# Two steps at a time in media attention and local attention of a decoder kernel on one core

## The chip, the core and the metric

The kernel runs on one core of one Trainium2 chip. The core has a matrix engine (TensorE, PE in the profile, with its weight loads as PEld), three engines for element-wise work (VectorE or DVE, ScalarE or ACT, GpSimd or POOL), and a queue that issues transfers (SyncE or SP). TensorE reads SBUF and writes PSUM, the accumulator memory; VectorE and ScalarE read PSUM. The metric is the time of one execution on the device in microseconds (us), lower is better. Of the kernel before there are three timed runs and one profiled execution.

## The reference, cut to what matters

The reference is two decoder layers on an input `x` of 8 batches of 512 rows and 256 columns, all in 32-bit floats. In order: self-attention, cross-attention to a context, two local transformer layers (each local attention and a feed-forward part), an attention in integers, an attention to the context as "media", and a mixture of eight experts. Each adds its result to `x`. The change touches two of them.

Local attention has 8 heads of 64 columns. A row attends to its own block of 128 rows and the block before:

```python
sim = jnp.einsum('bhwid,bhwjd->bhwij', bq, bk)
sim = jnp.where(mask, -jnp.finfo(sim.dtype).max, sim)
attn = jax.nn.softmax(sim, axis=-1)
out = jnp.einsum('bhwij,bhwjd->bhwid', attn, bv)
```

Queries and keys are normalised and rotated by position ahead of this. Media attention also has 8 heads of 64 columns; all 512 rows attend to all 512 rows of the context that the mask leaves:

```python
attn = jax.nn.softmax(sim, axis=-1)
out = jnp.einsum('bhij,bhjd->bhid', attn, v)
return out @ Wout
```

## The kernel before, in words

The stages run one after the other, with the beginning of each woven into the end of the one before. `x` stays in SBUF. Both attentions work transposed: keys stand on the partitions and queries along the columns, so that the exponentials are the operand of the value product as they come.

**A step.** Heads go in pairs, `c` = 0 to 3, since two heads of 64 fill 128 partitions. In media attention a step is a batch `b`, a pair of heads `c` and a block of 128 keys `kt`: 8 x 4 x 4 = 128 steps. In local attention it is a batch, a pair of heads and a half of the key blocks: 8 x 4 x 2 = 64 steps in each of two layers.

**Scores** (`scores`, lines 1912 and 2805). The two heads of a pair lie on the upper and the lower 64 partitions, so a score matmul uses 64 rows of the array, and the two run at once on two halves of its rows. They go to a PSUM tile `sc` of two banks, of which there are two. In media attention ScalarE takes the exponential from PSUM to `ma_e` (line 2817, four tiles), and the exponentials are summed over the key blocks in `ma_esum`: GpSimd copies the first (line 2823), VectorE adds the others (line 2825). In local attention VectorE adds the mask on the way from PSUM to `la_e` (line 1929, six tiles), and ScalarE takes the exponential in place (line 1933).

**Value products** (`weigh`, lines 1945 and 2827) take a step's exponentials two steps later. Each head has 64 value columns, so the two heads use two halves of the array's columns, and write the upper and lower half of one PSUM bank `po`, of which there is one. After the last step of a head pair ScalarE copies `po` out (lines 1962 and 2843). After two head pairs, sums over the exponentials are formed on 32-column tiles into the bank `sum` (recorded under lines 1940 and 2854), copied by VectorE, sent out through two small transfers, inverted (`inverted`, line 3162), spread over partitions by transfers into `x_wide` and multiplied on GpSimd (`times_rows`, line 3180). Media attention's last batch does the division on the chip instead (`spread_sums`).

**The rest.** Between steps stand two kinds of other work. `prepare` yields the next batch's work in small pieces: in media attention loads and normalisation, two groups of transposes (line 2784) and four projections of the queries (line 2794); in local attention two groups of transposes of `x` (`turn`, line 1796, copied by ScalarE to `la_hT`), twelve projections (line 1812), a rotation of queries and keys for each of four row tiles on VectorE (`rotate`, lines 1824 to 1846: some twenty instructions from the reduction `la_ss` to the last sum into `la_qk`), and the transposes of the rotated rows (`turn_heads`, line 1855, copied to `la_qkT`). All go through two PSUM banks `pj`. The other kind is `later`, a list of work with a delay counted in ticks: the inversion, the multiplication, the output projection (lines 1988 and 2892), and in media attention the routing for the experts (lines 2970 to 3063). `tick(n)` runs up to n pieces that are due.

**The order.** The loop of a stage is written out for all its steps:

```python
scores(i)
weigh(i - 2)

```

The order on each engine is made from this by a planner: on an engine the instruction that was written earliest goes first among those that are ready by the planner's estimate of times, so that an instruction that it thinks not ready is passed by later ones. At run time an engine does its instructions in the planned order and waits where one is not ready. `together(n)` (line 1448) wraps a group of matmuls: the first takes its place in the order, and the others follow it with the highest priority.

Of the kernel before, what the change touches and what calls it, by code (L numbers as in the profile page):

```python
# [27 lines left out]
F32 = mybir.dt.float32  # L28
# [5 lines left out]
AF = mybir.ActivationFunctionType  # L34
ALU = mybir.AluOpType
# [4 lines left out]
P = 128  # L40
B, S, C = 8, 512, 256
NST = S // P
# [1235 lines left out]
class FastDecoder(Decoder):  # L1278
# [480 lines left out]
    def local_attention(self, l, y, ahead):  # L1759
# [130 lines left out]
        with self.tc.tile_pool(  # L1890
# [11 lines left out]
            mask = self.alloc(pool, [P, NST, P], F32, "la_mask", bufs=1)  # L1902
# [7 lines left out]
            mask = mask.rearrange("p j k -> p (j k)")  # L1910

            def scores(n):
                b, rest = divmod(n, 8)
                c, half = divmod(rest, 2)
                d = held[b]
                ps = self.alloc(psum, [P, 2, 512], F32, "sc", bufs=2)
                for m in self.together(4):
                    jj, r = divmod(m, 2)
                    j = 2 * half + jj
                    to = min((j + 2) * P, S)  # L1920
                    rows = slice(64 * r, 64 * r + 64)
                    nc.tensor.matmul(  # L1922
                        ps[:, r, jj * 256 : jj * 256 + to - j * P],
                        d["qkT"][rows, 4 + c, j * P : (j + 1) * P], d["qkT"][rows, c, j * P : to],
                        start=True, stop=True,
                    )
                n_cols = 384 if half else 512
                ex = self.alloc(pool, [P, 2, 512], F32, "la_e", bufs=6)
                nc.vector.tensor_tensor(  # L1929
                    ex[:, :, :n_cols], ps[:, :, :n_cols],  # L1930
                    mask[:, :n_cols].unsqueeze(1).broadcast_to([P, 2, n_cols]), ALU.add,
                )
                nc.scalar.activation(ex[:, :, :n_cols], ex[:, :, :n_cols], AF.Exp, scale=-1.0)  # L1933
                d["e", rest] = ex

            def over_keys(out, lhsT, ex, half, jj):

# [5 lines left out]
                )  # L1943

            def weigh(n):
                b, rest = divmod(n, 8)
                c, half = divmod(rest, 2)
                d = held[b]
                if half == 0:
                    d["po"] = self.alloc(psum, [P, 512], F32, "po")  # L1950
                ex = d["e", rest]
                for m in self.together(4):
                    jj, r = divmod(m, 2)
                    at = 128 * c + 64 * r
                    over_keys(
                        d["po"][64 * r : 64 * r + 64, :], lambda j: d["v"][:, j, at : at + 64],
                        ex[:, r, :], half, jj,
                    )
                if half == 0:
                    return  # L1960
                o = d["o", c] = self.alloc(pool, [P, S], F32, "la_o", bufs=3)
                nc.scalar.copy(o, d["po"])  # L1962
                if c % 2 == 0:
                    return
                ps = self.alloc(psum, [P, 512], F32, "sum")
                for m in self.together(16):
                    hf, jj, r = m // 8, m // 4 % 2, m % 4
                    over_keys(
                        ps[32 * r : 32 * r + 32, :], lambda j: self.ones[:, :32],
                        d["e", 2 * (c - 1 + r // 2) + hf][:, r % 2, :], hf, jj,  # L1970
                    )
                total = self.alloc(pool, [P, S], F32, "la_total")
                nc.vector.tensor_copy(total, ps)
# [20 lines left out]

            n = 8 * B
            ahead.step()
            for i in range(n + 2):
                if i < n:
                    if i % 8 == 0:
                        ready = prepare(i // 8 + 1) if i // 8 + 1 < B else [()] * 8  # L2000
                    scores(i)
                if i >= 2:
                    weigh(i - 2)
                later.tick(1)
                if i < n:
                    for thunk in ready[i % 8]:
                        thunk()
                        later.tick(1)
                if i == n - 6:
                    early.close()  # L2010
                if i > n - 6:
                    ahead.step()
            ahead.step(100)
            later.drain()

# [732 lines left out]
    def stage_media_attention(self, w, out):  # L2748


        nc, t = self.nc, self.t
        wq, wkv, wo = w
        later = Background()
        with self.tc.tile_pool(reuse_waits="tile", name="ma", bufs=2) as pool, self.tc.tile_pool(
# [48 lines left out]
                    yield lambda g=g: project(d["q"], wq, d["xnT"], g)  # L2803

            def scores(n):
                b, rest = divmod(n, 16)
                c, kt = divmod(rest, 4)
                d = held[b]
                ps = self.alloc(psum, [P, 2, 512], F32, "sc", bufs=2)
                for r in self.together(2):  # L2810
                    rows = slice(64 * r, 64 * r + 64)
                    nc.tensor.matmul(  # L2812
                        ps[:, r, :], d["k"][rows, c, kt * P : (kt + 1) * P], d["q"][rows, c, :],
                        start=True, stop=True,
                    )
                ex = self.alloc(pool, [P, 2, 512], F32, "ma_e", bufs=4)
                nc.scalar.activation(  # L2817
                    ex, ps, AF.Exp, bias=bias[:, b * NST + kt : b * NST + kt + 1], scale=0.125
                )
                d[rest] = ex  # L2820
                if kt == 0:
                    d["sum", c] = self.alloc(pool, [P, 2, 512], F32, "ma_esum", bufs=3)
                    nc.gpsimd.tensor_copy(d["sum", c], ex)
                else:
                    nc.vector.tensor_tensor(d["sum", c], d["sum", c], ex, ALU.add)  # L2825

            def weigh(n):
                b, rest = divmod(n, 16)
                c, kt = divmod(rest, 4)
                d = held[b]  # L2830
                if kt == 0:
                    d["po"] = self.alloc(psum, [P, 512], F32, "po")
                ex = d.pop(rest)
                for r in self.together(2):
                    nc.tensor.matmul(  # L2835
                        d["po"][64 * r : 64 * r + 64, :],
                        d["v"][:, kt, 128 * c + 64 * r : 128 * c + 64 * r + 64], ex[:, r, :],
                        start=(kt == 0), stop=(kt == 3),
                    )
                if kt < 3:  # L2840
# [11 lines left out]
                ps = self.alloc(psum, [P, 512], F32, "sum")  # L2852
# [49 lines left out]
                thunk()  # L2902
            n = 16 * B
            ready = None
            for i in range(n + 2):
                if i < n:
                    if i % 16 == 0:
                        for thunk in ready or ():
                            thunk()
                        ready = prepare(i // 16 + 1) if i // 16 + 1 < B else iter(())  # L2910
# [534 lines left out]
```

## Time and profile before

| | |
|---|---|
| median of 3 runs | 3174.21 us (3169.55 to 3178.64) |
| profiled execution: time, span | 3162.05 us, 3160.1 us |
| TensorE matmuls | 2877.0 us, 91% of the span |
| VectorE | 2166.9 us, 69% |
| ScalarE | 1154.0 us, 37% |
| GpSimd | 408.7 us, 13% |
| granted TensorE clock, mean | 0.973 |

Shares are of the whole span; the stages differ. Local attention runs at about 740 to 1200 us and 1455 to 1905 us, media attention at about 2455 to 2885 us. A 32-bit matmul shows as two records, so the 256 score matmuls of media attention are 512 records of line 2812, and a step's group of two is four. A matmul's length in the profile contains its way through the array and its end is modelled: what a group costs is read from the start of one to the start of the next. In the rows of the profile a name such as `sc<-ma_qT,ma_kT` gives the tile written and the tiles read, and "64\*128" the rows and columns of the array in use.

### The profile page before, as it was taken

To read this page: it belongs to the slowest core of one execution; us is meant where nothing else is said; L and a number is where in the kernel's file an instruction comes from. 1 tells how busy PE (TensorE), PEld (TensorE's weight loads), DVE (VectorE), ACT (ScalarE), POOL (GpSimd) and SP (SyncE) were. 2 spreads that over 40 slices of the span, in tenths; PEclk is the share of its full clock that TensorE was granted. 3 is DMA by queue.
4 is the path that set the end of the run, shared out by engine and by line. 5 is a ranking of instruction groups with operands and counts; after the bars stand their busy time and mean duration, and the time that the engine had idled before them with its cause. 6 is when DMAs were issued, how large, how long until landed. Compare 5 with 4: busy or idle time off the path is not lost. (4 is left out here: it accounts for less than half of the span.)

```text
span 3160.1 us, 40243 instructions
## 1 busy us (share of the span) xinstructions
PE 2877.0 (91%) x14929; PEld 1485.8 (47%) x14944; DVE 2166.9 (69%) x4962; ACT 1154.0 (37%) x1607; POOL 408.7 (13%) x389
## 2 busy tenths in 40 slices
PE   8998888877998989999988989998796999997998
PEld 5642222224555556655555546654444233333665
DVE  7458888887788795357788798558787766566110
ACT  2146556653434431123434431113353444342111
POOL 1111000000011010000101111111201122222111
PEclk9999999989999999999999999999997999998999
DMA  7011111111000001001000011001332122213331
GB/s 237 1 53 44 54 57 48 32 24 51 16 21 22 19 27 42 0 1 35 22 15 21 22 44 61 15 12 60 95 127 94 41 79 103 75 64 103 102 138 59
DMA packets 130695, 168.73 MB, mean 53 GB/s; under 512 B 51760, under 2 KB 79665, under 8 KB 128442
## 3 DMA queue, kind: packets, MB, share of 16 engines
q1 hardware_dynamic: 126394, 154.48, 15.6%
q0 software_dynamic: 4096, 11.59, 1.0%
q8 instruction: 119, 1.95, 0.3%
q14 instruction: 86, 0.70, 0.1%
HBM read 113.12 MB, written 47.50 MB: 51 GB/s over the span
## 5 line engine op out<-in xcount | busy, mean ns | idle before, releaser
L1812 PE MATMUL pj<-w,la_hT 128*128 128x512 f32 x720 | 345.3, 612 | 23.9 <-DVE la_v L1817 21.9
L1664 DVE TENSOR_TENSOR x_e<-x_e,x_share 128x1024 f32<-128x1024 f32 x256 | 309.1, 1253 | 25.1 <-ACT x_e L1663 24.3
L1663 ACT ACTIVATE x_e<-sc 128x1024 f32<-128x1024 f32 x256 | 249.7, 1026 | 147.9 <-PE sc L1652 145.5
L2817 ACT ACTIVATE ma_e<-sc,ma_bias 128x1024 f32<-128x1024 f32 x128 | 142.4, 1114 | 198.8 <-PE sc L2812 185.5
L1812 PEld LDWEIGHTS pj<-w,la_hT 128*128 128x128 f32 x720 | 129.5, 191 | 167.0 <-issue 119.0
L3188 POOL TENSOR_TENSOR la_oT<-la_o,x_wide 128x512 f32<-128x512 f32 x64 | 96.8, 1523 | 790.6 <-DMA x_wide<-invs 654.6
L2825 DVE TENSOR_TENSOR ma_esum<-ma_esum,ma_e 128x1024 f32<-128x1024 f32 x96 | 122.8, 1280 | 91.6 <-ACT ma_e L2817 90.9
L1933 ACT ACTIVATE la_e<-la_e 128x1024 f32<-128x1024 f32 (+1 forms) x128 | 121.4, 951 | 175.2 <-DVE la_e L1929 175.2
L2146 ACT ACTIVATE lf_gate<-pj,lf_b 128x512 f32<-128x512 f32 (+1 forms) x82 | 56.3, 687 | 338.1 <-PE pj L2125 327.1
L1679 PE MATMUL po<-x_e,x_v 128*32 128x512 f32 x1024 | 140.1, 620 | 37.2 <-DVE x_e L1664 34.1
L2125 PE MATMUL pj<-lf_hnT,w 128*128 128x512 f32 (+1 forms) x368 | 171.9, 595 | 1.2 <-DVE lf_hid L2151 1.1
L1929 DVE TENSOR_TENSOR la_e<-sc,la_mask 128x1024 f32<-128x1024 f32 (+1 forms) x128 | 138.3, 1081 | 38.8 <-PE sc L1922 38.8
L1652 PE MATMUL sc<-x_q,x_k 32*128 32x512 f32 x1024 | 159.2, 662 | 0.3 <-ACT x_e L1663 0.2
L2125 PE MATMUL sc<-lf_hnT,w 128*128 128x512 f32 x336 | 158.0, 592 | 0.0
L2197 PE MATMUL po<-w,lf_hid 128*128 128x256 f32 x640 | 148.9, 379 | 0.2 <-DVE x L2207 0.2
L1988 PE MATMUL pj<-w,la_oT 128*128 128x256 f32 x512 | 124.4, 389 | 23.4 <-ACT la_qkT L1858 12.6
L2812 PE MATMUL sc<-ma_qT,ma_kT 64*128 64x512 f32 x512 | 145.2, 644 | 0.0
L2151 DVE SCALAR_TENSOR_TENSOR lf_hid<-sc,lf_b,lf_gate 128x512 f32<-128x512 f32 x70 | 52.4, 748 | 126.3 <-PE sc L2125 126.3
L2835 PE MATMUL po<-ma_e,ma_v 128*64 128x512 f32 x512 | 138.1, 618 | 0.0
L1940 PE MATMUL po<-la_e,la_v 128*64 128x256 f32 (+1 forms) x1024 | 129.1, 374 | 6.4 <-ACT la_o L1962 6.3
L1922 PE MATMUL sc<-la_qkT 64*128 64x256 f32 (+1 forms) x1024 | 132.6, 378 | 1.3 <-DVE la_e L1929 1.3
L1819 ACT ACTIVATE la_sq<-pj 128x512 f32<-128x512 f32 x120 | 71.4, 595 | 156.2 <-PE pj L1812 155.9
(491 smaller groups left out, 5264.5 us busy)
## 6 DMA issues: line engine op xcount, KB each, us to landing
x_wide<-invs SPq DMA_DIRECT2D x184, 128.0 KB
w<-in_f_w_dram SPq DMA_DIRECT2D x16, 1024.0 KB
kv<-kv_o SPq DMA_DIRECT2D x56, 256.0 KB
slots<-x_empty SPq DMA_DIRECT2D x8, 1028.0 KB
x_mask<-in_x_maskT_dram SPq DMA_DIRECT2D x8, 1024.0 KB
ma_kT<-kv SPq DMA_DIRECT2D x8, 1024.0 KB
ma_v<-kv SPq DMA_DIRECT2D x8, 1024.0 KB
ex_rows<-slots SPq DMA_DIRECT2D x7, 1028.0 KB
```

What stands on the lines that cost most here:

```text
L1652: nc.tensor.matmul(pair[r // 2][:, r % 2, :], d["k"][rows, g, kt * P : (kt + 1) * P], d["q"][rows, e, g, :], start=True, stop=True,)
L1663: nc.scalar.activation(ex, d["e"][rest][p], AF.Exp)
L1664: nc.vector.tensor_tensor(ex, ex, d["share"][:, kt, :].unsqueeze(1).broadcast_to([P, 2, 512]), ALU.mult)
L1679: nc.tensor.matmul(d["po"][32 * r : 32 * r + 32, :], d["v"][:, kt, 8 * g + 2 * r + e, :], ex[r // 2][:, r % 2, :], start=(kt == 0), stop=( ...
L1812: nc.tensor.matmul(ps, d["hT"][:, k, i * P : (i + 1) * P], wqkv[:, k, j * S : (j + 1) * S], start=(k == 0), stop=(k == 1),)
L1922: nc.tensor.matmul(ps[:, r, jj * 256 : jj * 256 + to - j * P], d["qkT"][rows, 4 + c, j * P : (j + 1) * P], d["qkT"][rows, c, j * P : to], ...
L1929: nc.vector.tensor_tensor(ex[:, :, :n_cols], ps[:, :, :n_cols], mask[:, :n_cols].unsqueeze(1).broadcast_to([P, 2, n_cols]), ALU.add,)
L2125: nc.tensor.matmul(ps[:m, :], w1[:, k, at : at + m], held[b]["hnT"][:, k, :], start=(k == 0), stop=(k == 1))
L2197: nc.tensor.matmul(ps[:, :C], held[b]["hid"][:, f, i * P : (i + 1) * P], w2[:, f, :], start=(f == 0), stop=False,)
L2812: nc.tensor.matmul(ps[:, r, :], d["k"][rows, c, kt * P : (kt + 1) * P], d["q"][rows, c, :], start=True, stop=True,)
L2817: nc.scalar.activation(ex, ps, AF.Exp, bias=bias[:, b * NST + kt : b * NST + kt + 1], scale=0.125)
L2835: nc.tensor.matmul(d["po"][64 * r : 64 * r + 64, :], d["v"][:, kt, 128 * c + 64 * r : 128 * c + 64 * r + 64], ex[:, r, :], start=(kt == 0) ...
```

## The change

Steps are taken in pairs. `scores` now takes the number of a pair, allocates both `sc` tiles at once, issues all matmuls of the two steps in one group, and then their mask additions, exponentials and sums. `weigh` takes the value products of both steps of the preceding pair in one group. In the loop the scores of a pair come first, then the value products of the pair before, and then the background pieces of both steps, with as many ticks as before. A pair is two key blocks of one head pair in media attention, and the two halves of one head pair in local attention. No tile is added, and no count of buffers changed. Of the diff, lines that only move in are left out:

```diff
@@ local_attention
             def scores(n):
-                b, rest = divmod(n, 8)
-                c, half = divmod(rest, 2)
+                b, c = divmod(n, 4)
                 d = held[b]
-                ps = self.alloc(psum, [P, 2, 512], F32, "sc", bufs=2)
-                for m in self.together(4):
-                    jj, r = divmod(m, 2)
+                both = [self.alloc(psum, [P, 2, 512], F32, "sc", bufs=2) for half in range(2)]
+                for m in self.together(8):
+                    half, jj, r = m // 4, m // 2 % 2, m % 2
                     j = 2 * half + jj
                     to = min((j + 2) * P, S)
                     rows = slice(64 * r, 64 * r + 64)
                     nc.tensor.matmul(
-                        ps[:, r, jj * 256 : jj * 256 + to - j * P],
+                        both[half][:, r, jj * 256 : jj * 256 + to - j * P],
                         d["qkT"][rows, 4 + c, j * P : (j + 1) * P], d["qkT"][rows, c, j * P : to],
                         start=True, stop=True,
                     )
+                for half, ps in enumerate(both):
+                    n_cols = 384 if half else 512
+                    ex = self.alloc(pool, [P, 2, 512], F32, "la_e", bufs=6)
...
             def weigh(n):
-                b, rest = divmod(n, 8)
-                c, half = divmod(rest, 2)
+                b, c = divmod(n, 4)
                 d = held[b]
-                if half == 0:
-                    d["po"] = self.alloc(psum, [P, 512], F32, "po")
-                ex = d["e", rest]
-                for m in self.together(4):
-                    jj, r = divmod(m, 2)
+                d["po"] = self.alloc(psum, [P, 512], F32, "po")
+                for m in self.together(8):
+                    half, jj, r = m // 4, m // 2 % 2, m % 2
...
-                if half == 0:
-                    return
...
             n = 8 * B
             ahead.step()
-            for i in range(n + 2):
-                if i < n:
-                    if i % 8 == 0:
-                        ready = prepare(i // 8 + 1) if i // 8 + 1 < B else [()] * 8
-                    scores(i)
-                if i >= 2:
-                    weigh(i - 2)
-                later.tick(1)
-                if i < n:
-                    for thunk in ready[i % 8]:
-                        thunk()
-                        later.tick(1)
-                if i == n - 6:
-                    early.close()
-                if i > n - 6:
-                    ahead.step()
+            for pair in range(0, n + 2, 2):
+                if pair < n:
+                    if pair % 8 == 0:
+                        ready = prepare(pair // 8 + 1) if pair // 8 + 1 < B else [()] * 8
+                    scores(pair // 2)
+                if pair >= 2:
+                    weigh(pair // 2 - 1)
+                for i in (pair, pair + 1):
+                    later.tick(1)
+                    if i < n:
+                        for thunk in ready[i % 8]:
+                            thunk()
+                            later.tick(1)
+                    if i == n - 6:
+                        early.close()
+                    if i > n - 6:
+                        ahead.step()
@@ stage_media_attention
             def scores(n):
-                b, rest = divmod(n, 16)
-                c, kt = divmod(rest, 4)
+                b, rest = divmod(n, 8)
+                c, kts = rest // 2, (2 * (rest % 2), 2 * (rest % 2) + 1)
                 d = held[b]
-                ps = self.alloc(psum, [P, 2, 512], F32, "sc", bufs=2)
-                for r in self.together(2):
+                both = [self.alloc(psum, [P, 2, 512], F32, "sc", bufs=2) for kt in kts]
+                for m in self.together(4):
+                    kt, r = kts[m // 2], m % 2
...
+                for kt, ps in zip(kts, both):
+                    ex = d[4 * c + kt] = self.alloc(pool, [P, 2, 512], F32, "ma_e", bufs=4)
...
             def weigh(n):
-                b, rest = divmod(n, 16)
-                c, kt = divmod(rest, 4)
+                b, rest = divmod(n, 8)
+                c, kts = rest // 2, (2 * (rest % 2), 2 * (rest % 2) + 1)
...
-                ex = d.pop(rest)
-                for r in self.together(2):
+                exs = [d.pop(4 * c + kt) for kt in kts]
+                for m in self.together(4):
+                    kt, r = kts[m // 2], m % 2
...
-            for i in range(n + 2):
-                if i < n:
-                    if i % 16 == 0:
...
-                    scores(i)
-                if i >= 2:
-                    weigh(i - 2)
-                if i % 16 > 0:
-                    thunk = next(ready, None)
-                    if thunk is not None:
-                        thunk()
-                later.tick(2)
+            for pair in range(0, n + 2, 2):
+                if pair < n:
+                    if pair % 16 == 0:
...
+                    scores(pair // 2)
+                if pair >= 2:
+                    weigh(pair // 2 - 1)
+                for i in (pair, pair + 1):
+                    if i % 16 > 0:
+                        thunk = next(ready, None)
+                        if thunk is not None:
+                            thunk()
+                    later.tick(2)
```

More of the change, by code (lines that the diff above doesn't have):

```diff
@@ L1926, in scores @@
                     )
[L1927 to L1934, printed above, removed]
+                for half, ps in enumerate(both):
+                    n_cols = 384 if half else 512
+                    ex = self.alloc(pool, [P, 2, 512], F32, "la_e", bufs=6)
+                    nc.vector.tensor_tensor(
+                        ex[:, :, :n_cols], ps[:, :, :n_cols],
+                        mask[:, :n_cols].unsqueeze(1).broadcast_to([P, 2, n_cols]), ALU.add,
+                    )
+                    nc.scalar.activation(ex[:, :, :n_cols], ex[:, :, :n_cols], AF.Exp, scale=-1.0)
+                    d["e", 2 * c + half] = ex
             def over_keys(out, lhsT, ex, half, jj):
@@ L1956, in weigh @@
                         d["po"][64 * r : 64 * r + 64, :], lambda j: d["v"][:, j, at : at + 64],
-                        ex[:, r, :], half, jj,
+                        d["e", 2 * c + half][:, r, :], half, jj,
                     )
-                if half == 0:
-                    return
                 o = d["o", c] = self.alloc(pool, [P, S], F32, "la_o", bufs=3)
@@ L2811, in scores @@
                     rows = slice(64 * r, 64 * r + 64)
                     nc.tensor.matmul(
-                        ps[:, r, :], d["k"][rows, c, kt * P : (kt + 1) * P], d["q"][rows, c, :],
+                        both[m // 2][:, r, :], d["k"][rows, c, kt * P : (kt + 1) * P], d["q"][rows, c, :],
                         start=True, stop=True,
                     )
[L2816 to L2825, printed above, removed]
+                for kt, ps in zip(kts, both):
+                    ex = d[4 * c + kt] = self.alloc(pool, [P, 2, 512], F32, "ma_e", bufs=4)
+                    nc.scalar.activation(
+                        ex, ps, AF.Exp, bias=bias[:, b * NST + kt : b * NST + kt + 1], scale=0.125
+                    )
+                    if kt == 0:
+                        d["sum", c] = self.alloc(pool, [P, 2, 512], F32, "ma_esum", bufs=3)
+                        nc.gpsimd.tensor_copy(d["sum", c], ex)
+                    else:
+                        nc.vector.tensor_tensor(d["sum", c], d["sum", c], ex, ALU.add)
@@ L2827, in weigh @@
             def weigh(n):
-                b, rest = divmod(n, 16)
-                c, kt = divmod(rest, 4)
+                b, rest = divmod(n, 8)
+                c, kts = rest // 2, (2 * (rest % 2), 2 * (rest % 2) + 1)
                 d = held[b]
-                if kt == 0:
+                if kts[0] == 0:
                     d["po"] = self.alloc(psum, [P, 512], F32, "po")
-                ex = d.pop(rest)
-                for r in self.together(2):
+                exs = [d.pop(4 * c + kt) for kt in kts]
@@ L2835, in weigh @@
+                for m in self.together(4):
+                    kt, r = kts[m // 2], m % 2
                     nc.tensor.matmul(
                         d["po"][64 * r : 64 * r + 64, :],
-                        d["v"][:, kt, 128 * c + 64 * r : 128 * c + 64 * r + 64], ex[:, r, :],
+                        d["v"][:, kt, 128 * c + 64 * r : 128 * c + 64 * r + 64], exs[m // 2][:, r, :],
                         start=(kt == 0), stop=(kt == 3),
                     )
-                if kt < 3:
+                if kts[1] < 3:
@@ L2904, in stage_media_attention @@
             ready = None
-            for i in range(n + 2):
-                if i < n:
-                    if i % 16 == 0:
+            for pair in range(0, n + 2, 2):
+                if pair < n:
+                    if pair % 16 == 0:
                         for thunk in ready or ():
                             thunk()
-                        ready = prepare(i // 16 + 1) if i // 16 + 1 < B else iter(())
-                    scores(i)
-                if i >= 2:
-                    weigh(i - 2)
-                if i % 16 > 0:
-                    thunk = next(ready, None)
-                    if thunk is not None:
-                        thunk()
-                later.tick(2)
+                        ready = prepare(pair // 16 + 1) if pair // 16 + 1 < B else iter(())
+                    scores(pair // 2)
[7 more added lines that the diff above has]
+                    later.tick(2)
             later.drain()
```

## The prediction

> **What bounds the kernel now.** I read the page's first part, then each changed stage's window, then who waits for whom inside it. The page gives TensorE the largest share, but its busy time is no measure of what the stage would gain. The windows are local attention of layer 0, of layer 1, and media attention:
>
> ```profile
> 740.00:1200.00 460.00, 419.69 (x2434) 234.40 (x2435) 381.69 (x896) 180.52 (x286) 49.86 (x45) 0.99 0.09 26
> 1455.00:1905.00 450.00, 407.89 (x2377) 224.34 (x2375) 374.31 (x857) 178.28 (x283) 47.13 (x43) 0.99 0.08 25
> 2455.00:2885.00 430.00, 425.73 (x1745) 157.64 (x1745) 286.82 (x708) 176.32 (x196) 106.06 (x98) 1.00 0.21 71
> ```
>
> The columns are matmul, weight load, VectorE, ScalarE, GpSimd. In media matmuls fill 426 of 430 us; in local attention VectorE fills 83%. Media's chain of work in order of time, columns start and length, is TensorE alone:
>
> ```profile
> 2620.94 1.91 PE pj L2794 x4
> 2622.86 1.06 PE sc L2812 x4
> 2623.91 1.01 PE po L2835 x4
> 2624.92 1.91 PE pj L2794 x4
> ...
> 2634.80 1.06 PE sc L2812 x4
> 2635.86 1.01 PE po L2835 x4
> 2636.87 1.06 PE sc L2812 x4
> 2637.93 1.01 PE po L2835 x4
> ```
>
> A step is scores (sc, on 64-row tiles of the array), value products (po, on 64-column tiles), then the rest (pj, the whole array). What would the same matmuls cost without changing tiles? The timeline of local attention has eight full-array matmuls of the same 512 columns in a row (columns start, modelled length):
>
> ```profile
> 1006.76 1.99 PE L1988 MATMUL pj<-w,la_oT 128*128 128x256 f32 x8
> 1008.59 3.60 PE L1812 MATMUL pj<-w,la_hT 128*128 128x512 f32 x8
> 1012.02 0.60 PE L1855 MATMUL pj<-ident,la_qk 128*128 128x128 f32 x4
> ```
>
> From start to start, (1012.02 - 1008.59) / 8 = 0.429 us each. A score group has four matmul records, two at a time: 2 x 0.429 = 0.858, and it takes 1.06. So 0.20 us of each score group, 0.15 of each value group (1.01) and 0.19 of a projection (1.91 - 4 x 0.429) is the price of entering and leaving a tile shape. The trace has one place where two stretches of one shape already touch: in media's last batch a value group is followed by sums on the same 64-column tiles.
>
> ```profile
> 2881.36 1.08 PE L2835 MATMUL po<-ma_e,ma_v 128*64 128x512 f32 x4
> 2882.27 1.03 PE L2876 MATMUL sum<-ma_esum,ones 128*64 128x512 f32 x4
> ```
>
> There the value group takes 0.91 from start to start, not 1.01. The price is per stretch, not per group.
>
> Local attention is another matter. VectorE's timeline at the turn of a batch (idle time in brackets) shows:
>
> ```profile
> 965.32 1.23 DVE L1846 TENSOR_TENSOR la_qk<-la_qk,la_r 128x1024 f32<-128x1024 f32 x1
> 966.46 0.68 DVE L1817 COPY la_v<-pj 128x512 f32<-128x512 f32 x1
> 967.06 1.21 DVE L1929 TENSOR_TENSOR la_e<-sc,la_mask 128x1024 f32<-128x1024 f32 x1
> 970.80 0.96 DVE L1929 TENSOR_TENSOR la_e<-sc,la_mask 128x768 f32<-128x768 f32 x1 [2.52 <-PE sc L1922]
> 975.18 0.69 DVE L1973 COPY la_total<-sum 128x512 f32<-128x512 f32 x1 [3.43 <-PE sum L1940]
> 977.69 1.22 DVE L1828 TENSOR_REDUCE la_ss<-la_sq 128x16 f32<-128x1024 f32 x1 [1.82 <-ACT la_sq L1819]
> ```
>
> The rotation of a batch's last rows ends at 966.55 and the next batch's first begins at 977.69. Outside this stretch of 11.1 us VectorE hardly stops in the 58.5 us of a batch, and TensorE waits for it (1.97 us ahead of the transposes at 966.69). So a batch is some 47 us set by VectorE and 11 set by TensorE; only in the latter, and in each layer's last batch, which rotates nothing, does TensorE's time count.
>
> **What the Trainium skill says.** TensorEngine Tiling (Array Packing), Key Properties: changing the tiling mode, not merely the tile, drains TensorE. TensorE: Matmul & The Clock Gate, LDWEIGHTS, puts a weight load at its columns over 1.2 GHz: 0.107 us for 128 columns, 0.053 for 64. The trace agrees: the first matmul of a score stretch is followed 0.53 us later instead of 0.43, of a value stretch after 0.47, and each stretch is left some 0.09 to 0.10 late. The same page, under the architectural detail, has ScalarE and VectorE as strict FIFOs; their in-order waits above fit. The skill's first page, Performance Expectations, calls matmul busy time a bad metric; local attention's 91% beside a VectorE that paces it bears that out.
>
> **The change, part by part.** It adds no arithmetic: every matmul, exponential, mask addition, copy and DMA stays. It joins stretches.
>
> Media has 128 steps, so 64 pairs. Score stretches fall from 128 to 64: 64 x 0.20 = 12.9 us. Value stretches likewise: 64 x 0.15 = 9.7. In the order of before there are 78 stretches of rest; these lie in 57 of the 64 pairs, so some 20 fewer, at 0.15 (transposes, 0.59 less 4 x 0.109) to 0.19 each: 3.4. Sum 26.0 us, all on the chain above. What could take it back: the two `sc` tiles of a pair are the two that there are, so the next pair's scores need both exponentials of this one. They run 1.11 us each, after each half; the second ends some 1.06 + 0.86 + 1.3 = 3.3 us into a pair of 430 / 64 = 6.7 us. Hidden, with 3 us to spare; without that cover it would be 64 x 1.1 = 70 us. `ma_e` (four tiles) and the single `po` tile are released at the same distance or earlier, since the value products of the pair before still stand between.
>
> Local attention has 32 pairs a layer. The last batch is scores and value products in turn, on TensorE: 4 x (0.21 + 0.16) = 1.5 us a layer, 3.0 for both. In the seven others the 11.1 us count. Before, TensorE does there transposes, value products, transposes, scores, projection, value products and sums, projections. The joined order has the same work in about three fewer stretches: -0.55 us. But the second score group now needs the keys and queries of the last rows, which ScalarE copies until 968.5, and score group one no longer stands between the turn of `x` (ends 969.8) and the projection that reads its copies (ScalarE ends them at 970.6): up to 0.85 us uncovered unless sums or value products fill it. Bounds per batch: -0.55, and -0.55 + 0.85 + 0.8 (wait for the copies) + 1.0 (a score group that filled the wait before the transposes and now comes after them) = +2.1; times 14 batches, -8 to +29. I take 0, since value products and sums are ready and can stand in both gaps. If instead VectorE did not pace the rest, a layer would gain 32 x (0.21 + 0.16) + 40 x 0.17 = 18.6, two 37.
>
> What else moves: the first step's rest now comes behind the second step's scores and the value products. On GpSimd the copy that starts `ma_esum` (1.04 us) moves ahead of the first step's multiplications and row copies; GpSimd is 25% busy. On SP the two small DMAs of the sums are issued by the value products, so about a step earlier, ahead of the first step's `x_wide` loads; they wait for the copy of the sums, and `x_wide` behind them would be late by less than a step, 3.4 us. Those products are used four ticks later, and GpSimd already waits 331.7 us for them in local attention at no cost to TensorE. Uncovered, each of 8 x 2 in a stage would cost that step. I put both at nothing.
>
> Sum: 26.0 + 3.0 + 0 = 29 us. The profiled execution took 3162.05 us for a span of 3160.1; it becomes 3133. The median of the runs is 3174.21, 12 above it, and the same step gives 3145.
>
> **The rivals.** *B, all of it counts:* local attention is set by TensorE after all. For: its 91%. Against: VectorE's idle time lies in one place. 26 + 37 = 63 off, 3111. *C, local attention gives it back:* the upper bound above, +29, against 29: 3174. For: the pair's scores and the projections are the uncovered steps. Against: value products and sums are ready. *D, slower:* the same stretch at the turn of a batch, with ScalarE's queue on top. The copies of the turned `x` stand behind both exponentials of the pair, and so behind two mask additions (1.21 + 0.96 us) on VectorE: about 1 us more, 3.1 a batch, 44 in all, less 29: 3189. It decides from (29 + 9.5) / 14 = 2.75 us a batch. Against: VectorE is idle just there. *E, the pairs aren't kept:* the order on an engine is the planner's, and it may split a group whose second half is not ready by its estimate. For: in local attention rest already stands between scores and value products of one step. Against: media kept its order exactly. Then about 5 us, 3169.
>
> **How the numbers follow.** The forecast, media's 24 to 28 with local attention between -11 and +6, has 0.52 and its own range of 3137 to 3156. B 0.16, C 0.10, D 0.15, E 0.07. A measurement of this kernel tells some 0.3%, 9.5 us, from no change. Forecast and B are faster: 0.68. C and E are within: 0.17. D is slower: 0.15. The range from 3109 to 3178 holds forecast, B but for its edge, C and E, and leaves out D.
>
> **What would show it.** In media's chain: sc x8 of about 1.92 us, then po x8 of 1.87, half as many stretches, a stage of some 404 us instead of 430. In local attention: the gap between the last rotation and the next batch's first reduction still near 11 us, and the stage shorter by a few us only. Against it: sc groups of four as before, new waits for `ma_e`, `ma_o` or `la_qkT` in front of scores, or a gap of over 13 us at the turn of a batch.

## The result and the profile after

The changed kernel takes 3141.43 us, median of four runs (3141.04 to 3142.42), beside 3172.30 for four runs of the kernel before. The ratio is 0.990, with a 95% interval of 0.9883 to 0.9918: about 31 us less. The forecast was 3145. Its total is right; the split behind it is not, as the profile and the experiments show.

The page's first line of engines, of the kernel after (busy us, share of the span, instructions):

```profile
span 3140.5 us, 40216 instructions
PE 2861.4 (91%) x14944; PEld 1511.3 (48%) x14944; DVE 2156.3 (69%) x4962; ACT 1146.1 (36%) x1607; POOL 401.6 (13%) x389
```

VectorE, ScalarE, GpSimd and the weight loads have the instruction counts of before; TensorE is busy 15.6 us less. The profiled execution took 3142.42 us, 19.6 less than the profiled one of before, which lay 12 under its own median. Start to local attention is 4.2 us longer, in stages that the change does not touch. From the first scores of local attention in layer 0 to those in layer 1 it is 4.9 us shorter, from there to media's first scores 15.2, and from these to the end 3.7. So most of the gain lies where the forecast put next to nothing, and media, where it put 26, gives little: from first scores to last value product 420.7 us instead of 426.6.

Media's window of after, moved to its own times (matmul, weight load, VectorE, ScalarE, GpSimd):

```profile
2440.00:2865.00 425.00, 404.59 (x1744) 171.79 (x1741) 294.90 (x699) 172.42 (x195) 106.51 (x98) 0.99 0.22 72
```

Matmuls there now leave 20 us of 425 uncovered; before they left 4 of 430. The chain of work of after in media, in order of time, shows where (start, length):

```profile
2613.66 1.99 PE pj L2791 x4
2615.64 1.92 PE sc L2811 x8
2617.56 1.87 PE po L2835 x8
2619.43 1.00 PE sum L2854 x8
2620.42 3.65 PE pj L2892 x16
2624.07 1.92 PE sc L2811 x8
2625.99 1.87 PE po L2835 x8
2627.86 3.67 PE pj L2892 x16
...
2631.55 0.43 DVE x L2897
...
2633.20 1.14 DVE mo_ln_rstd L1460
...
2634.36 0.95 DVE mo_ln_t L1462
...
2636.92 0.42 DVE mo_rows L157
...
2637.39 1.30 PE pj L2992 x4
2638.69 1.92 PE sc L2811 x8
```

The groups of eight are there, at 1.92 and 1.87 us, the forecast's numbers to the digit. But the chain, TensorE alone before, now goes over VectorE once a batch: the last projection is added to `x` (line 2897), the routing takes its statistics and normalises (lines 143 to 157), and its transposes (line 2992) wait for that. The waits of TensorE in media attention of after have it as the largest (total us, times, longest):

```profile
PE pj L2992 <- DVE mo_rows L157: 13.2, 7, 2.4
```

TensorE's timeline of after shows one of the seven (start, modelled length, in brackets the idle time before):

```profile
2631.44 1.99 PE L2811 MATMUL sc<-ma_qT,ma_kT 64*128 64x512 f32 x8
2633.36 1.94 PE L2835 MATMUL po<-ma_e,ma_v 128*64 128x512 f32 x8
2637.39 1.30 PE L2992 MATMUL pj<-ident,mo_rows 128*128 128x128 f32 x4 [2.09 <-DVE mo_rows L157]
```

One pair's scores and value products, 3.8 us, are all that stands between the addition to `x` and the transposes, and VectorE needs 5.8 us from the start of that addition until the first rows are ready.

In local attention VectorE's timeline at the turn of a batch, after:

```profile
971.94 1.23 DVE L1846 TENSOR_TENSOR la_qk<-la_qk,la_r 128x1024 f32<-128x1024 f32 x1
973.08 0.69 DVE L1969 COPY la_total<-sum 128x512 f32<-128x512 f32 x1
975.76 0.96 DVE L1930 TENSOR_TENSOR la_e<-sc,la_mask 128x768 f32<-128x768 f32 x1 [2.00 <-PE sc L1922]
977.03 0.25 DVE L3175 RECIPROCAL x_inv<-x_sums 128x16 f32<-128x16 f32 x1 [0.31 <-DMA x_sums<-sums]
978.40 2.09 DVE L1930 TENSOR_TENSOR la_e<-sc,la_mask 128x1024 f32<-128x1024 f32 x2 [1.12 <-PE sc L1922]
982.94 0.69 DVE L1969 COPY la_total<-sum 128x512 f32<-128x512 f32 x1 [2.45 <-PE sum L1941]
986.33 1.22 DVE L1828 TENSOR_REDUCE la_ss<-la_sq 128x16 f32<-128x1024 f32 x1 [2.70 <-ACT la_sq L1819]
```

From the last rotation's end (973.17) to the next batch's first reduction it is now 13.2 us, 2.0 longer, just as the forecast's upper bound had it. Yet the batch that ends here took 57.3 us from first reduction to first reduction, where the one that ends at the turn shown for the kernel before took 58.1. From the third of these intervals in a layer on, before has 58.1 to 60.4 us (mean 59.2) and after 57.3, one of 58.5 apart. The first two were shorter before, 51.5 to 57.5 against 54.0 to 57.5, but counted by the batches' first scores all six after the first are shorter on average, 59.5 to 58.0 us in layer 0 and 59.1 to 57.6 in layer 1.

The longer turn costs nothing, because time only moved there: VectorE is idle for 11.09 us in the batch of before and in the batch of after, and does 88 instructions in both. The turn took over one mask addition, one copy of sums and a reciprocal, and gave up a copy of `la_v`. What made the batch shorter, with the same arithmetic and the same idle time? One instruction in VectorE's timeline of before, in the middle of a rotation, stands out:

```profile
957.64 0.17 DVE L1463 TENSOR_TENSOR la_rt<-la_rt,la_ss 128x16 f32<-128x16 f32 x1
958.26 1.21 DVE L1463 TENSOR_TENSOR la_rt<-la_rt,la_ss 128x16 f32<-128x16 f32 x1
```

The same operation of the same shape, 0.17 and 1.21 us. GpSimd's timeline of before at that time has its multiplication by the inverted sums (`times_rows`), which ends at the same moment:

```profile
958.17 1.27 POOL L3188 TENSOR_TENSOR la_oT<-la_o,x_wide 128x512 f32<-128x512 f32 x1 [24.99 <-DMA x_wide<-invs]
```

I counted VectorE's instructions that last over 0.2 us longer than the lower quartile of those of the same operation and shape, from a stage's first scores to its last value product. In the kernel before there are 26 in layer 0 (21.9 us over) and 28 in layer 1 (25.8); after, 15 (15.9) and 14 (14.9). Every one overlaps an instruction of GpSimd. Batch by batch they are the whole difference: in layer 0 of before, batches of 58.5, 58.1 and 59.2 us hold four each, 3.2, 2.9 and 4.0 us over, which leaves 55.3, 55.2 and 55.2; after, a batch of 57.3 holds two, 2.1 over, which leaves 55.2.

Why two and not four? GpSimd's timeline of after at the turn shown above has two of the batch's four multiplications:

```profile
983.15 2.50 POOL L3189 TENSOR_TENSOR la_oT<-la_o,x_wide 128x512 f32<-128x512 f32 x2 [14.23 <-DMA x_wide<-invs]
```

They run while VectorE, done with the copy of sums at 983.63, waits until 986.33 for its next reduction, and so lengthen nothing. Of a layer's 28 or 29 multiplications 12 lie in a turn after the change; before, 2 in layer 0 and none in layer 1.

So there were two accounts to tell apart. **The forecast's:** media gives 26, local attention 3, and the two traces differ from it by the scatter of single executions. **The traces':** media gives 5 to 9, because its gain goes into a wait for the routing; local attention gives 20 to 27, because VectorE's instructions meet GpSimd's less often.

### The profile page after: what moved, and what is told of

The parts are those of the page before. It is cut to its first block, busy times and chain, and to the rows that moved or that the text cites. A ratio compares the mean times of both kernels' runs of the same rounds, so it can differ in the third digit from the quotient of the medians.

```text
span 3140.5 us, 40216 instructions
## 1 busy us (share of the span) xinstructions
PE 2861.4 (91%) x14944; PEld 1511.3 (48%) x14944; DVE 2156.3 (69%) x4962; ACT 1146.1 (36%) x1607; POOL 401.6 (13%) x389
## 5 line engine op out<-in xcount | busy, mean ns | idle before, releaser
L2817 ACT ACTIVATE ma_e<-sc,ma_bias 128x1024 f32<-128x1024 f32 x128 | 135.7, 1110 | 164.9 <-PE sc L2811 163.4
L2824 DVE TENSOR_TENSOR ma_esum<-ma_esum,ma_e 128x1024 f32<-128x1024 f32 x96 | 129.1, 1346 | 71.6 <-ACT ma_e L2817 35.6
L3189 POOL TENSOR_TENSOR la_oT<-la_o,x_wide 128x512 f32<-128x512 f32 x64 | 87.3, 1372 | 572.7 <-DMA x_wide<-invs 410.4
L1922 PE MATMUL sc<-la_qkT 64*128 64x256 f32 (+1 forms) x1024 | 122.8, 370 | 13.1 <-ACT la_qkT L1858 11.3
L2811 PE MATMUL sc<-ma_qT,ma_kT 64*128 64x512 f32 x512 | 129.6, 625 | 0.0
L2194 PEld LDWEIGHTS po<-w,lf_hid 128*128 128x128 f32 x640 | 117.8, 190 | 20.3 <-issue 6.7
L2835 PE MATMUL po<-ma_e,ma_v 128*64 128x512 f32 x512 | 124.3, 606 | 0.0
```

What stands on the lines that cost most here:

```text
L2194: nc.tensor.matmul(ps[:, :C], held[b]["hid"][:, f, i * P : (i + 1) * P], w2[:, f, :], start=(f == 0), stop=False,)
L2811: nc.tensor.matmul(both[m // 2][:, r, :], d["k"][rows, c, kt * P : (kt + 1) * P], d["q"][rows, c, :], start=True, stop=True,)
L2817: nc.scalar.activation(ex, ps, AF.Exp, bias=bias[:, b * NST + kt : b * NST + kt + 1], scale=0.125)
L2835: nc.tensor.matmul(d["po"][64 * r : 64 * r + 64, :], d["v"][:, kt, 128 * c + 64 * r : 128 * c + 64 * r + 64], exs[m // 2][:, r, :], start= ...
```

## The experiments

**Pairs in media alone.** Local attention's loop, `scores` and `weigh` are those of before (the diff is against the kernel after):

```diff
@@ local_attention (back to the kernel before)
-            for pair in range(0, n + 2, 2):
...
+            for i in range(n + 2):
+                if i < n:
+                    if i % 8 == 0:
+                        ready = prepare(i // 8 + 1) if i // 8 + 1 < B else [()] * 8
+                    scores(i)
+                if i >= 2:
+                    weigh(i - 2)
```

> Pairs in media attention alone; local attention as before. The forecast's account (joined stretches save 26 us in media, 3 in local attention): about 26 us less than before, 3146. The account read from the two traces (media saves the stretches, but gives some 20 us back in waits for VectorE ahead of the routing's transposes; the larger part of the whole gain is local attention's): 5 to 9 us less, about 3165, with 7 waits of 2.2 to 2.6 us ahead of these transposes.

Measured: 3163.52 us, ratio 0.9984 (0.9974 to 0.9994) to 3169.31 of before: 6 us less. The waits ahead of the routing's transposes are there, seven of 13.8 us together.

**Pairs in local attention alone**, the other half of the change, with media's functions and loop as before.

> Pairs in local attention alone; media attention as before. The forecast's account: about 3 us less than before, 3169. The account read from the two traces: 20 to 27 us less, about 3148, with batches of local attention of 57.3 us instead of 58 to 60.

Measured: 3143.80 us, 0.9917 (0.9902 to 0.9932): 26 us less, with full batches of 57.3 us. The two parts add up to 31, the whole change. The traces' account holds and the forecast's split falls: the two sizes are nearly the reverse of what was forecast.

**The routing two ticks later**, with the pairs in both. If media's gain of joining is real and only a wait consumes it, then more matmuls between the addition to `x` and the transposes must bring it out:

```diff
             later.add(1, stats)
             later.add(2, norm)
-            later.add(3, lambda: turn(0))
-            later.add(4, lambda: turn(1))
-            later.add(5, logits)
-            later.add(6, choose)
-            later.add(8, count)
-            later.add(9, place)
+            later.add(5, lambda: turn(0))
+            later.add(6, lambda: turn(1))
+            later.add(7, logits)
+            later.add(8, choose)
+            later.add(10, count)
+            later.add(11, place)
             for i in range(NST):
-                later.add(10 + i, lambda i=i: send(i))
+                later.add(12 + i, lambda i=i: send(i))
```

> The kernel after with the routing's pieces, from its first transposes on, due two ticks (one pair) later. If the joined background put the transposes too near to the normalisation that they read: the waits of 2.2 to 2.6 us ahead of them go, 7 times, so 15 us less than the kernel after, about 3126. If the wait is for VectorE as a whole, which is merely late: it reappears before the next transposes or projections, and the time stays within 3 us of 3141.

Measured: 3124.78 us (3117.38 to 3131.68), 0.9865 (0.9847 to 0.9884): 16.7 less than after, or 13.6 when each is set against the kernel before as measured beside it (44.5 and 30.9 less), and the fastest of the kernels here that compute the whole reference. Media's batches, from the third on, take 50.8 to 51.1 us instead of 54.1 to 55.3, and its chain is TensorE alone again:

```profile
2645.04 1.92 PE sc L2811 x8
2646.96 1.87 PE po L2835 x8
2648.83 3.63 PE pj L2791 x8
2652.46 1.92 PE sc L2811 x8
2654.38 1.87 PE po L2835 x8
2656.24 0.99 PE sum L2854 x8
2657.24 1.93 PE pj L2892 x8
```

**The same with only the joining undone.** Media's scores and value products of a pair come in turn, and both rests after them; the routing stays late:

```diff
+                for i in (pair, pair + 1):
+                    if i < n:
+                        scores(i)
+                    if i >= 2:
+                        weigh(i - 2)
                 for i in (pair, pair + 1):
                     if i % 16 > 0:
                         thunk = next(ready, None)
```

> As the run with the late routing, but in media attention the scores and value products of a pair stand in turn, each in a group of its own (scores, values, scores, values, then the rest of both steps), so that only the joining of their stretches is undone. Price per stretch: 64 x (0.20 + 0.15) = 22.6 us more than the run with the late routing. If what counts is only where the background stands: the same time within 3 us.

Measured: 3140.42 us (3131.41 to 3146.81), 0.991 (0.9893 to 0.9927), 15.6 above the joined kernel. Its chain in media:

```profile
2648.01 1.06 PE sc L2809 x4
2649.07 1.01 PE po L2832 x4
2650.08 3.63 PE pj L2791 x8
...
2654.07 1.06 PE sc L2809 x4
2655.13 1.01 PE po L2832 x4
2656.14 1.06 PE sc L2809 x4
2657.20 1.01 PE po L2832 x4
2658.21 3.63 PE pj L2791 x8
```

A batch takes 53.9 us, 2.85 more than joined (forecast of the price for scores and value products: 8 x 0.20 + 8 x 0.15 = 2.8). Over eight batches that is 22.8, as expected; the medians differ by 7 less. With intervals of some 6 us either way on each of the two, 22.8 is not excluded. In the two profiles, 14.0 apart, media from its first scores to the end differs by 18.5, and 4.5 of that had been made up in the stages ahead, which the edit does not touch. For a finer comparison I took each matmul record's time from its start to the start of the next one and summed by line, from the first scores of media's batch 0 to those of batch 7 (worked out from the traces, us):

| | before | after | routing late | late, apart |
|---|---|---|---|---|
| scores, 56 pairs | 120.5 | 111.8 | 109.5 | 121.5 |
| value products | 111.2 | 116.4 | 102.7 | 111.2 |
| projections of the queries | 53.6 | 52.5 | 50.6 | 50.6 |
| transposes of the routing | 9.7 | 10.5 | 5.2 | 5.2 |
| all lines | 371.4 | 367.6 | 343.7 | 364.6 |

A wait shows at the record ahead of it, so the 13.7 us between after's value products and those with the routing late are the waits for the routing. Of the 5.3 us between the transposes 1.0 is a group of eight that falls past the end of the count; the other 4 are VectorE's four normalisations, 1.38 us together, that pace four transposes (1.30 us in the chain above, 0.13 each where nothing holds them). Without the waits, scores and value products of 56 pairs take 19.5 us less than before; 56 x 0.35 = 19.6 was forecast.

**The routing later, without pairs**, that is, the kernel before with the same delays:

> The kernel before, without pairs, with the routing's pieces in media attention due two steps later. If only the joined background put the routing's transposes too near to their normalisation: nothing to gain here but the 0.4 to 0.5 us that they wait for in each of 7 batches, so within 5 us of the kernel before, and batches of media attention of 54.5 to 55 us. If a late routing is worth most of what the pairs with late routing gained in media attention (4 us a batch): batches of about 52 us and 20 us less.

Measured: 3176.12 us beside 3167.38, 1.0015 (0.9994 to 1.0036), no gain; batches of 54.5 to 55.0 us. In the window of the table its matmuls take 367.3 us, 4.1 less than before's 371.4, all of it at the routing's transposes (5.6 for 9.7; 1.0 of that is again a group of eight past the end of the count), which no longer follow the pace of the normalisations. But in the profiles it is 708.4 us from media's first scores to the end, 704.8 before. So the delay is no saving by itself. It restores what the pairs took away.

**Later, but for the last two batches**, whose routing nothing can hide behind:

```diff
+            more = 2 if b < B - 2 else 0
-            later.add(5, lambda: turn(0))
...
+            later.add(3 + more, lambda: turn(0))
```

> As the run with the late routing, but the last two batches keep the old delays, since their routing stands at the end, where nothing covers it (from the last output projection of media attention to the end 271.2 us with the late routing, 268.4 in the kernel after). If the late routing costs its delay there: about 3 us less than the run with the late routing, 3122. If not: the same within 1.5 us.

Measured: 3125.57 us (3121.32 to 3127.24), 0.9862 (0.9837 to 0.9887), the same as with all eight late. From media's last projection to the end it is 271.1 us, with all eight late 271.2, in the kernel after 268.4. The expected few us are not there: the last two batches' delay is not what costs the 2.8 us at the end. All four kernels with a late routing have 271.0 to 271.2 there, the six others 268.0 to 270.0; why is open.

**No multiplication on GpSimd in local attention.** To test whether GpSimd's work lengthens VectorE's, the multiplication by the inverted sums becomes a copy on ScalarE, which leaves the division out. First in the kernel before (`undivided` is true in local attention's calls alone):

```diff
+        if undivided:
+            later.add(2, lambda: nc.scalar.copy(out, o))
+            return
         later.add(2, lambda: nc.gpsimd.tensor_tensor(out, o, wide, ALU.mult))
```

> The kernel before with the multiplication by the inverted sums left out of local attention: ScalarE copies the values instead of GpSimd multiplying them, so the output of local attention is not divided. If GpSimd's multiplications lengthen VectorE's instructions (26 and 28 in the two layers of before, 22 and 26 us), and VectorE paces local attention: batches of 56 to 57 us instead of 58 to 60 and 25 to 35 us less in all. If they do not pace it: batches as before and within 5 us of it.

Measured: 3111.76 us beside 3171.02, 0.98 (0.9776 to 0.9823): 59 us less, twice what was expected. No instruction of VectorE is lengthened any more. Two lines of VectorE's instructions on `la_ss`, from 755 to 1110 us, show it (times, then shortest, median and longest in ns). Before:

```profile
L1463 DVE TENSOR_TENSOR la_rt<-la_rt,la_ss x75: 127/174/1277, 756.3 to 1100.3; 128x16 f32<-128x16 f32 x75
L1460 DVE TENSOR_SCALAR la_rn<-la_ss x26: 162/174/1250, 755.9 to 1109.2; 128x16 int32<-128x16 int32 x26
```

The kernel before, without the multiplication:

```profile
L1463 DVE TENSOR_TENSOR la_rt<-la_rt,la_ss x79: 130/174/176, 763.9 to 1109.8; 128x16 f32<-128x16 f32 x79
L1460 DVE TENSOR_SCALAR la_rn<-la_ss x27: 163/174/176, 763.5 to 1108.9; 128x16 int32<-128x16 int32 x27
```

In the same window the changed kernel stands between them, with one of the two lines freed:

```profile
L1463 DVE TENSOR_TENSOR la_rt<-la_rt,la_ss x75: 126/174/179, 760.5 to 1105.3; 128x16 f32<-128x16 f32 x75
L1460 DVE TENSOR_SCALAR la_rn<-la_ss x25: 160/174/1241, 760.1 to 1103.6; 128x16 int32<-128x16 int32 x25
```

Full batches take 55.3 us, what was left of those of before without their lengthening. The lengthening was 21.9 + 25.8 = 47.7 us; in the profiles the two stages, from first scores to last value product, are 51.9 us shorter. The other 11 of the 59 are not settled (the copy on ScalarE also no longer waits for `x_wide`).

**The same in the kernel after:**

> The kernel after with the same multiplication left out of local attention. If local attention gained by pairs because fewer of VectorE's instructions meet a multiplication on GpSimd: its batches are within 0.5 us of those of the run without pairs and the two layers together differ by under 8 us. If it gained by fewer changes of the tile shape on TensorE: the batches stay 1.5 us or more shorter than without pairs, 20 us in both layers.

Measured: 3113.57 us, 0.9818 (0.9797 to 0.9839), 1.8 above the one before it, and batches of 55.2 us. With GpSimd's multiplication out, the pairs gain nothing on balance in a kernel whose media part alone gives 6. In the profiles local attention ends 3.2 and 4.4 us sooner per layer with pairs, but from the first scores of a stage to those of the next it is 683.4 us with pairs against 682.1 without, and 973.9 against 971.8: what follows takes back all of it. So local attention's gain from pairs hangs on GpSimd's multiplication.

## Why the prediction was right in sum, and where it was wrong

**Price of a stretch: right.** 1.92 and 1.87 us for groups of eight, 19.5 us for 56 pairs where 19.6 was forecast, and 2.85 us a batch when only the joining is undone. The rest gave its share too: the projections of the queries fell by 3.0 us over seven batches, where 3.4 over eight was forecast for all the stretches of rest. The prediction's "The trace agrees" on weight loads rests on the starts of the matmuls; the loads' own records last 0.19 and 0.13 us (lines 2812 and 2835 of before, median), longer than the 0.107 and 0.053 cited there, and the measurement decides. No sum used either.

**Media's 26 us: the sum right, its arrival wrong.** The step that failed is "Sum 26.0 us, all on the chain above", with the list of what could take it back. That list looked at tiles of PSUM and at exponentials. The moved rest was weighed on GpSimd and SP only, and VectorE was left out. The routing's pieces are due 1, 2 and 3 ticks after the last projection is added to `x`. The number of ticks is the same, as said ahead, but a pair's ticks now follow each other with no matmuls between. Before, three steps of scores and value products, 3 x 2.07 = 6.2 us, covered VectorE's 5.8 us but for 0.4 to 0.6 a batch; after, one pair of 3.8 us does. By the table the change keeps 371.4 - 367.6 = 3.8 us, where pairs bring 367.3 - 343.7 = 23.6 when the routing is late in both kernels. Freed from it, media gives 23.8 us from its first scores to the end in the profile.

**Local attention's 3 us and nothing: the reasons right, the number wrong.** VectorE does pace a batch, joining does not matter there (55.3 and 55.2 us with GpSimd's multiplication out), and the gap grew by 2.0 us, the upper bound. The failing step is "I put both at nothing", said of GpSimd's work with the reason that it waits "at no cost to TensorE": it asked whether GpSimd would be late, not whom its instructions slow, and took the 47 us "set by VectorE" as given. The trace of before had the answer: `la_rt` of 0.17 us lasts up to 1.28. The time missed was 23 us, 26 less the 3 forecast; the count of lengthened instructions shows 17 of it (47.7 less 30.8).

**The total** came out at 3141 for 3145 because an expected gain of 20 was absent from media and an unexpected one of about the same size turned up in local attention. It proves neither.

**The rivals.** *B* had local attention gain, but as TensorE's time; batches of 55.3 and 55.2 us refute its reason, and 3111 was not reached. *C* and *D* fall with the local part's 26 us gain; the longer turn of *C* did come, 2.0 us a batch, and did not decide. *E* falls where it counted: the groups of media are whole. In local attention 14 of 64 score groups were split. The sign named as speaking against the forecast, a gap of over 13 us, appeared, and was the wrong sign to watch: the gap took over work and idle time of VectorE's from the rest of the batch. No rival had the wait that did cost media its gain.

**Not settled.** What puts two multiplications into the turn when steps are paired is traced only as far as the transfers of `x_wide` that they wait for; no kernel moved the multiplications alone. The 9 us of local attention's 26 that the count does not show go with the multiplication too, since without it pairs gain nothing there, but no run shares them out. The waits for `la_o`, which the multiplication holds, are too small: TensorE's were 6.4 us in the two stages before and 5.0 after. And unchanged stages vary by up to 8 us between executions (742.9 to 750.8 us from the start to local attention), so a difference of this size between two profiles is no evidence.

## What to carry to other kernels

Joining stretches of one tile shape paid its price per stretch here where TensorE sets the time (19.5 us for 19.6), once whatever was timed by the old order is spaced anew: background work that is due in counted ticks keeps its count and loses the matmuls between when ticks bunch. Trace from the last result that a stage produces to the first matmul that needs it, on every engine between, and set the matmuls that still stand there against it. Where an element-wise engine sets the time, ask whether another engine makes its instructions longer. And check a right total part by part, in kernels that have one part each, before believing its reasons.

## What the hardware showed

A short instruction of VectorE can last as long as the GpSimd instruction that it meets: 0.17 us became 1.21 beside a multiplication of 1.27 us. In the kernel before 26 and 28 instructions were lengthened so in a stage of some 430 us, and none in local attention when GpSimd's multiplications were gone. The Trainium skill, GPSIMD Engine Reference, in its Specifications and Key points, says that the two engines share their SBUF interfaces and contend where VectorE has two SBUF inputs or is in a two-port mode. The traces agree for `la_rt<-la_rt,la_ss`, with two inputs; they show it as well for `la_rn<-la_ss` (line 1460, 0.17 us to 1.25), which has one tile as its input, and do not tell whether that one ran in a two-port mode. In the two stages before, 63 instructions of VectorE began inside one of local attention's multiplications, over 0.15 us ahead of its end. Of the 55 that read SBUF alone 54 were lengthened; of the 8 that read PSUM none, such as six copies `la_v<-pj` of 0.68 us. In media attention of after two of the routing's instructions last 1.14 and 0.95 us in the chain above, where the second one's line takes 0.16 a microsecond later. VectorE's busy time contains all this: fewer such meetings make it less busy with the same instructions, and of its time in the two stages 47.7 us were lengthening before, 30.8 after.
